# Layer 0's experts on gathered 256-row tiles between the scan tiles, and the end of layer 0 batch by batch

## The chip, the cores and the metric

The kernel runs on one core of a Trainium2 chip. A core has five engines that work side by side and meet through semaphores: TensorE (PE, matrix products), VectorE (DVE), ScalarE (ACT), GpSimd (POOL) and SyncE (SP), which here only issues transfers. Sixteen DMA engines carry the transfers of all of them. Each engine works off its own list of instructions in order. The metric is the device time of one execution in microseconds (us); the median of the runs is what counts, and lower is better.

## What is computed

Four layers, each of the form x + s(xn) * silu(g(xn)), where xn is the layer norm of x. Only layer 0 and the joint to layer 1 matter here. In layer 0, s is a selective scan (Mamba) and g a mixture of eight experts of which each row takes two:

```python
xz = x @ in_proj_w.T + in_proj_b              # x: 4 batches x 512 rows x 128
x_part, z = split(xz)                         # 256 channels each
x_conv = silu(causal_conv4(x_part))
dt = softplus(x_conv @ dt_w.T + dt_b);  Bm, Cm = x_conv @ B_w.T + B_b, x_conv @ C_w.T + C_b
h[t] = exp(dt[t] * A) * h[t-1] + dt[t] * Bm[t] * x_conv[t]     # 16 states per channel
y = (sum_s h[t] * Cm[t] + D * x_conv[t]) * silu(z);   s = y @ out_w.T + out_b

logits = xn @ gate_w + gate_b;  top 2 of 8, softmax over the two -> comb
h = gelu(xn @ w1[e] + b1[e])                  # 128 -> 512, exact GELU
g = sum_e comb[:, e] * (h @ w2[e] + b2[e])    # 512 -> 128
```

That is 2048 rows; each row needs two of the eight experts. Layer 1 is an attention of 16 heads beside four experts (again two per row).

## The kernel before

Everything is float32 in tiles of 128 partitions. The instructions of layer 0 are written in the order in which each engine is to take them (`manual_schedule`), so where a call stands in the loop decides what it waits behind.

**The scan loop.** The 4 batches x 256 channels x 16 states are cut into 128 tiles of 128 partitions (8 channels x 16 states) by 512 time steps, the tiles n = 0 to 127, 32 of them to a batch. A tile needs dt and dt*x of its 8 channels, each repeated 16 times over the partitions: two loads `rep` of 256 KB (`fetch`, L690, on SP) from the DRAM buffer `ddd`. ACT makes exp(A*dt) (`decay`, L696, tile `dA`), DVE multiplies B with the other load (`drive`, L703, `dBx`) and runs the recurrence (`scan`, L707, `hs`, two buffers), POOL multiplies by C (L709, `hc`). Every four steps `sum_states` (L718) has PE sum the states. `decay` runs LEAD + 1 = 6 steps ahead of the scan; the loads run AHEAD = 4 tiles ahead of their users, in 4 and 5 buffers. The next batch's projection, convolution and step sizes (`project_in`, `convolve`, `silus`, `in_stages`) and the last one's output (`gated`, `back`) are placed at set steps through `after(steps, fn, ...)`, a table of calls for later steps.

**The experts of layer 0.** `Experts` runs all eight experts on all rows: 32 steps of 512 rows (8 experts x 4 batches), two of them every eight scan steps. `hidden` (L562, L563) does four matmuls of 128 x 512 and four GELUs, `output` (L573) 16 matmuls of 128 columns, and `add_weighted` (L523) adds each of the four row blocks to `acc`, weighted with the gate. `weighted_bias` starts `acc` with the biases. ACT loads a table before the GELUs and another after them (`exp_ln`, L746).

**The end of layer 0.** `end_layer0` takes silu of all of `acc`, multiplies and adds into x; `begin_layer` norms all 16 row blocks and transposes them for layer 1.

**Layer 1.** Its four experts are already routed: class `Routed` computes each row's place (`route`), scatters the rows into the DRAM buffer `xs1` by 32 indirect transfers (L1257, on POOL), takes 19 tiles of 256 rows through their expert, whose weights come by an indirect load (L1270, on POOL), stores them to `ys` and gathers two rows per row again (`results`, L1346). Its stages run beside the attention through `Places`: `add` puts a chain of stages on a list, `work` and `place` run one stage each when its turn has come, `need` runs a chain to its end. The rows of `xs1` are filled with zeros by 19 stores at scan steps 40 to 58. At attention step PAUSE = 36 the attention stops for the experts.

Of the kernel before, what the change touches and what calls it, by code (L numbers as in the profile page):

```python
# [34 lines left out]
E0, FF0 = 8, 512  # L35
E1, FF1 = 4, 704
# [3 lines left out]
SLOT1 = 256  # L40
TILES1 = (2 * N - E1) // SLOT1 + E1
# [9 lines left out]
for _name, _n in (  # L51
    ("in_b", 4), ("conv_w", 2 * KCONV), ("conv_b", 2), ("dt_b", 2), ("A_log", 2 * STATE), ("D", 2),
    ("B_b", 1), ("C_b", 1), ("b1_0", E0 * 4), ("b1_2", E2 // 2), ("b1_3", E3 * 2), ("b2_3", E3), ("q_b", 1), ("k_b", 1),
):
    _COLS[_name] = (_at, _n)
    _at += _n
# [15 lines left out]
for _name, _n in (("before", P), ("ones", P), ("tile", TILES1), ("full", N // SLOT1), ("carry", E1 * NC), ("part", 1)):  # L72
    _RT[_name] = (_at, _n)
    _at += _n
# [3 lines left out]
def _constants():  # L78
# [24 lines left out]
    for name, v in (  # L103
        ("before", i[:, None] < i[None, :]), ("ones", 1.0), ("tile", np.arange(TILES1)),
        ("full", SLOT1 * np.arange(N // SLOT1)), ("carry", np.tile(np.arange(NC) > 0, E1)),
        ("part", i[:, None]),
    ):
        at, n = _RT[name]
        route[:, at : at + n] = v
# [40 lines left out]
def _layout(a):  # L150
# [26 lines left out]
    put("b1_0", chunked(a["L0_ffn_b1"].reshape(-1), E0 * 4))  # L177
# [38 lines left out]
    for i, w1, w2 in ((0, "w1", "w2"), (1, "w1", "w2"), (2, "w1", "w2"), (3, "W1", "W2")):  # L216
        out[f"f{i}_w1"], out[f"f{i}_w2"] = a[f"L{i}_ffn_{w1}"], a[f"L{i}_ffn_{w2}"]
# [11 lines left out]
def kernel(ctx: ExitStack, tc: tile.TileContext, ap: dict):  # L229
# [59 lines left out]
    xs1 = dram.tile([TILES1 * SLOT1, D], F32, name="xs1")  # L289
# [3 lines left out]
    nc.sync.dma_start(out=pick2, in_=ap["c_pick2"])  # L293

# [140 lines left out]
    def begin_layer(s):  # L435

        normalize(s, x)
        xnT = keep.tile([P, N], F32, name="xnT")
        transpose_chunks(xnT, s, NC)
        return xnT  # L440

    def end_layer0(s, y):

        act.activation(y, y, AF.Silu)
        half = NC // 2
        for h in range(2):
            cs = slice(h * half, (h + 1) * half)
            dve.tensor_tensor(s[:, cs, :], s[:, cs, :], y[:, cs, :], ALU.mult)
            dve.tensor_tensor(x[:, cs, :], x[:, cs, :], s[:, cs, :], ALU.add)

# [51 lines left out]
    def weighted_bias(acc, cw, b2, e, fp):  # L502

        for q in range(NC // 4):
# [3 lines left out]
            cwT = fp.tile([e, 512], F32, tag="cwT", name="cwT", bufs=1)  # L508
# [5 lines left out]

    def add_weighted(acc, py, cw, tb, e, first=False):

        for i in range(4):
            c = 4 * tb + i
            src = py[:, i * P : (i + 1) * P]
            if first:  # L520
                dve.tensor_scalar(acc[:, c, :], src, cw[:, c, e : e + 1], None, ALU.mult)
            else:
                dve.scalar_tensor_tensor(acc[:, c, :], src, cw[:, c, e : e + 1], acc[:, c, :], ALU.mult, ALU.add)  # L523


    def moe0_gate(xnT, scratch):
# [9 lines left out]
        yield cw  # L536

    class Experts:


        def __init__(self, fp, xnT, cw, acc):
            self.fp, self.xnT, self.cw, self.acc = fp, xnT, cw, acc
            self.steps = [(e, tb) for e in range(E0) for tb in range(4)]
            self.w, self.h = {}, {}

        def load(self, e):
            if e < E0 and e not in self.w:
                w1 = self.fp.tile([P, FF0], F32, tag="w1", name="w1")
                nc.sync.dma_start(out=w1, in_=ap["f0_w1"][e])
                w2 = self.fp.tile([P, 4, D], F32, tag="w2", name="w2")  # L550
                nc.sync.dma_start(out=w2, in_=ap["f0_w2"][e].rearrange("(f p) d -> p f d", p=P))
                self.w[e] = (w1, w2)

        def hidden(self, k):
            e, tb = self.steps[k]
            if tb == 2:
                self.load(e + 1)
            w1 = self.w[e][0]
            h = self.fp.tile([P, 4, 512], F32, tag="h", name="h", bufs=3)
            for f in range(4):  # L560
                ph = bank()
                pe.matmul(ph, w1[:, f * P : (f + 1) * P], self.xnT[:, tb * L : (tb + 1) * L], start=True, stop=True)  # L562
                act.activation(h[:, f, :], ph, AF.Gelu, bias=col("b1_0", e * 4 + f))  # L563
            self.h[k] = h

        def output(self, k):
            e, tb = self.steps[k]
            h, w2 = self.h.pop(k), self.w[e][1]
            py = bank("py")
            for i in range(4):  # L570
                cs = slice(i * P, (i + 1) * P)
                for f in range(4):
                    pe.matmul(py[:, cs], h[:, f, cs], w2[:, f, :], start=(f == 0), stop=(f == 3))  # L573
            return lambda: add_weighted(self.acc, py, self.cw, tb, e)


    def layer0(ctx0, mp, fp, s_out, acc):
# [23 lines left out]
        xnT = keep.tile([P, N], F32, name="xnT")  # L601
        at, n = _COLS["A_log"]
        A = mp.tile([P, n], F32, name="A")
        ln = tc.tile_pool(name="ln0", bufs=1)
        ln_pool = ln.__enter__()
        ln_close = lambda: ln.__exit__(None, None, None)
# [29 lines left out]
        def step_size(b, o):  # L636
# [6 lines left out]
            dd = mp.tile([P, 2, L], F32, tag="dd", name="dd", bufs=2)  # L643
# [498 lines left out]

# [646 lines left out]
```

## Time and profile before

| | us |
|---|---|
| runs, median of 3 (lowest to highest) | 1801.49 (1791.64 to 1809.43) |
| profiled execution, its own time | 1814.22 |
| its span, first to last instruction | 1812.5 |
| mean granted TensorE clock | 0.828 |
| busy PE, DVE, ACT, POOL over the span | 1373.3, 1143.7, 955.1, 536.2 |
| first scan instruction starts | 53.63 |
| last scan instruction ends | about 489 |
| first score row of layer 1 reduced on DVE | 531.91 |
| last scatter of layer 1's rows starts | 668.8 |
| layer 1's expert matmuls start | 691.9 |

How lines of the profile are read: a group names the line of the kernel, the engine, the operation, what is written and read and in what shapes, and how often; then the busy time in us and the mean of one in ns; then the idle time of the engine just before it, and who ended that. A wait reads: who waited, for whom, us in total, how often, the longest. A window row gives busy time and number of instructions for each engine. SPq is SP's DMA queue, PEld TensorE's weight loads.

### The profile page before, as it was taken

The page shows a single profiled execution, that of the slowest core. Times are in us where ns is not written, and L with a number is a line of the kernel's source. Part 1 is how long each engine was busy: PE and PEld are TensorE (multiplying, and loading weights), DVE is VectorE, ACT ScalarE, POOL GpSimd, SP SyncE. Part 2 cuts the span into 40 slices and gives each one's busy share as a digit, 9 for nine tenths or more (in the row PEclk, how much of TensorE's full clock was granted, in tenths as well). Part 3 has the DMA queues.
Part 4 walks back from the last instruction along what each step waited for, and adds up shares of the span by engine and source line. Part 5 has one row for each costly group of instructions (what it writes and reads, how often), then busy time and mean ns, then how long its engine had stood idle before and what let it go on. Part 6 is the DMA issues. An engine that isn't in the chain of part 4 may idle for free.

```text
span 1812.5 us, 22587 instructions
## 1 busy us (share of the span) xinstructions
PE 1373.3 (76%) x7845; PEld 699.2 (39%) x7845; DVE 1143.7 (63%) x1987; ACT 955.1 (53%) x1302; POOL 536.2 (30%) x513
## 2 busy tenths in 40 slices
PE   4678878788857888999586667776767877788771
PEld 2445445445532336888232222222312322233331
DVE  6467677677766664222466775657658799876422
ACT  3555655555524654223335777777885545354640
POOL 1245354444514652111534221214010101031223
PEclk8689889898857878999677877778868898598985
DMA  4557677576321231441302231220310211112112
GB/s 125 144 160 196 157 211 193 141 209 179 99 56 35 44 101 50 142 158 39 72 18 51 39 51 23 40 31 13 58 24 13 86 27 19 18 31 65 45 44 75
DMA packets 119122, 148.64 MB, mean 82 GB/s; under 512 B 15384, under 2 KB 79968, under 8 KB 117216
## 3 DMA queue, kind: packets, MB, share of 16 engines
q1 hardware_dynamic: 112048, 122.55, 28.7%
q0 software_dynamic: 6960, 24.65, 4.0%
q8 instruction: 62, 1.02, 0.2%
q14 instruction: 52, 0.43, 0.1%
HBM read 113.84 MB, written 16.01 MB: 72 GB/s over the span
## 4 chain that ended last, share of the span: by engine, by line
PE 43%; DVE 20%; ACT 15%; issue 10%; DMA 6%; POOL 3%; SPq 1%; POOLq 0%; DVEq 0%; ACTq 0%
PE wide L878 6%; PE py L1032 6%; PE wide L1313 5%; PE bank L562 5%; ACT at L1016 4%; PE py L573 4%; PE wide L885 3%; DMA rep<-ddd 3%; DVE nm L985 3%; PE py L1293 3%; ACT ep L980 3%; DVE den L981 2%; DVE hs L707 2%; PE wide L927 1%; ACT dA L696 1%
## 5 line engine op out<-in xcount | busy, mean ns | idle before, releaser
L1016 ACT ACTIVATE at<-wide 128x1024 f32<-128x1024 f32 (+3 forms) x384 | 352.5, 923 | 265.1 <-PE wide L885 175.6
L985 DVE TENSOR_REDUCE nm<-wide 128x2 f32<-128x1024 f32 (+3 forms) x256 | 256.8, 1019 | 105.1 <-PE wide L885 88.7
L1032 PE MATMUL py<-at,vaug 128*32 128x512 f32 (+3 forms) x1536 | 235.8, 671 | 11.7 <-POOL at L1020 8.5
L709 POOL TENSOR_TENSOR hc<-hs,C 128x512 f32<-128x512 f32 x128 | 163.2, 1279 | 250.3 <-DVE hs L707 145.1
L981 DVE TENSOR_REDUCE den<-ep 128x2 f32<-128x1024 f32 x128 | 155.5, 1217 | 115.0 <-ACT ep L980 114.3
L878 PE MATMUL wide<-k,q 48*128 48x512 bf16 (+4 forms) x768 | 167.9, 413 | 78.1 <-ACT at L1016 42.3
L562 PE MATMUL bank<-xnT,w 128*128 128x512 f32 x256 | 149.3, 738 | 75.7 <-ACT h L563 56.9
L980 ACT ACTIVATE ep<-wide 128x1024 f32<-128x1024 f32 x128 | 132.7, 1037 | 43.5 <-PE wide L878 33.9
L707 DVE TENSOR_TENSOR_SCAN hs<-dA,dBx 128x512 f32<-128x512 f32 x128 | 154.7, 1209 | 0.6 <-POOL hc L709 0.6
L573 PE MATMUL py<-w,h 128*128 128x128 f32 x1024 | 129.5, 288 | 19.6 <-DVE acc L523 19.6
L573 PEld LDWEIGHTS py<-w,h 128*128 128x128 f32 x1024 | 127.3, 204 | 38.6 <-DVE acc L523 27.9
L885 PE MATMUL wide<-own_bf 128*128 128x128 bf16 x880 | 138.8, 245 | 0.0
L696 ACT ACTIVATE dA<-rep,A 128x512 f32<-128x512 f32 x128 | 87.3, 715 | 97.6 <-DVE hs L707 69.4
L878 PE MATMUL wide<-q,k 63*128 63x512 bf16 (+3 forms) x512 | 101.9, 393 | 40.3 <-DVE nm L985 16.2
L703 DVE TENSOR_TENSOR dBx<-B,rep 128x512 f32<-128x512 f32 x128 | 89.0, 696 | 55.5 <-DMA rep<-ddd 35.8
L562 PEld LDWEIGHTS bank<-xnT,w 128*128 128x128 f32 x256 | 58.0, 237 | 166.6 <-ACT h L563 77.5
L878 PEld LDWEIGHTS <-q 48*128 48x128 bf16 (+1 forms) x768 | 49.8, 96 | 163.1 <-issue 145.3
L1313 PE MATMUL wide<-xT,w 128*128 128x256 f32 x456 | 108.5, 387 | 2.1 <-ACT h L1316 1.5
L1318 DVE TENSOR_TENSOR h<-h,wide 128x512 f32<-128x512 f32 x57 | 39.2, 688 | 110.5 <-ACT h L1316 110.5
L563 ACT ACTIVATE h<-bank,cols 128x512 f32<-128x512 f32 x128 | 84.7, 687 | 42.6 <-PE bank L562 42.2
L885 PEld LDWEIGHTS <-own_bf 128*128 128x128 bf16 x880 | 52.2, 101 | 113.8 <-issue 107.3
L878 PE MATMUL wide<-qr,kr 48*128 48x512 bf16 x256 | 61.3, 452 | 45.3 <-ACT ep L980 40.1
(324 smaller groups left out, 2086.7 us busy)
## 6 DMA issues: line engine op xcount, KB each, us to landing
rep<-ddd SPq DMA_DIRECT2D x256, 256.0 KB
q<-parts SPq DMA_DIRECT2D x192, 48.0 KB
k<-parts SPq DMA_DIRECT2D x192, 48.0 KB
w<-in_f_w_dram SPq DMA_DIRECT2D x18, 256.0 KB
ddd<-dd POOLq DMA_DIRECT2D x8, 512.0 KB
w<-in_f_w_dram SPq DMA_DIRECT2D x32, 128.0 KB
qr<-rparts SPq DMA_DIRECT2D x64, 48.0 KB
kr<-rparts SPq DMA_DIRECT2D x64, 48.0 KB
```

The source lines that it names most:

```text
L562: pe.matmul(ph, w1[:, f * P : (f + 1) * P], self.xnT[:, tb * L : (tb + 1) * L], start=True, stop=True)
L573: pe.matmul(py[:, cs], h[:, f, cs], w2[:, f, :], start=(f == 0), stop=(f == 3))
L707: dve.tensor_tensor_scan(h, st[n]["dA"], st[n]["dBx"], 0.0, ALU.mult, ALU.add)
L709: pool.tensor_tensor(hc, h, batch[tiles[n][0]]["C"], ALU.mult)
L878: pe.matmul(ps[:, j, lo:hi], lhs[m][r, cs], rhs[m][r, lo:hi], start=True, stop=not own)
L885: pe.matmul(ps[:, j, cs], lhs_own, rhs_own, start=False, stop=True)
L980: act.activation(e, ps, AF.Exp)
L981: dve.tensor_reduce(s["den"][:, qc, 2 * m : 2 * m + 2], e, AX.X, ALU.add)
L985: dve.tensor_reduce(s["nm"][:, qc, 2 * m : 2 * m + 2], ps[:, :, :hi], AX.X, ALU.max, negate=True)
L1016: act.activation(a[:, :, lo:], ps[:, :, lo:], AF.Exp)
L1032: pe.matmul(s["po"][32 * j : 32 * j + 32, lo:], vaug[b % 2][:, kc, 4 * g + j, :], a[:, j, lo:], start=kc == 0, stop=kc == 3,)
L1313: pe.matmul(ph[:, g, m * SLOT1 : (m + 1) * SLOT1], wk[:, f + g, m, :], self.x[k], start=True, stop=True)
```

## The change

Layer 0's experts are routed as layer 1's are. `Routed` becomes a common class, with `Routed0` and `Routed1` for what differs; its own table of constants is loaded at the start. Layer 0 has 23 tiles of 256 rows (the most that 4096 choices over eight experts can need). The scratch `xs` is shared by both layers and filled with zeros once, by one transfer at the start, issued by POOL. In the scan loop:

- the route stages run one per step from step 0, then the 32 scatters, one per step (`places.work()` is called twice per step); `places.need("rows")` at step 43 makes sure of them, and the first two tiles are loaded there;
- from step FIRST = 46, two tiles every five steps: rows transposed by PE and copied by ACT, then both first layers, then the second layers in the two steps after, each with a copy on ACT and a store on SP. Loads of the next tiles (weights by POOL, rows by SP) stand one and three steps after the pair begins;
- from step DONE = 108 the results of the batches one after the other, a stage per step: two stages of four gathers, then the weighted sum on DVE onto the biases in `acc`, and silu in three stages; after each, `turn` multiplies, adds into x, norms and transposes that batch. Batch 3's results come after the loop, and the turns of batches 2 and 3 in layer 1's first attention steps.

Layer 1's routing waits until all four turns are over. `end_layer0`, `begin_layer`, `Experts` and `add_weighted` go. `hc` has 6 buffers instead of 8 and `dd` one instead of two; `sum_states` runs at n % 4 == 1 instead of 3.

```diff
+    xs = dram.tile([TILES0 * SLOT, D], F32, name="xs")
+    pool.dma_start(
+        out=xs.rearrange("(p k) d -> p k d", p=P), in_=zero[:, None, :].to_broadcast([P, TILES0 * SLOT // P, D])
+    )
...
+        def load(self, k):
+            if k < self.tiles:
+                pool.indirect_dma_start(
+                    out=self.w[k % len(self.w)], out_offset=None, in_=self.weights,
+                    in_offset=bass.IndirectOffsetOnAxis(ap=self.expert[:, k : k + 1], axis=0),
+                    bounds_check=self.e * P - 1, oob_is_err=False,
+                )
+                self.x[k] = self.wp.tile([P, 2, D], F32, tag="xr", name="xr", bufs=3)
+                nc.sync.dma_start(
+                    out=self.x[k], in_=xs[k * SLOT : (k + 1) * SLOT, :].rearrange("(h p) d -> p h d", p=P)
+                )
...
+        def results(self, b, y, room, biased=False):
+            ya = room()
+            yb = room() if biased else None
+            own = lambda c: yb[:, c, :] if biased else y[:, 4 * b + c, :]
+            for c in range(4):
+                self.gather(own(c), 0, 4 * b + c)
+                self.gather(ya[:, c, :], 1, 4 * b + c)
+                if c % 2:
+                    yield 0
+            yield 0
+            for c in range(4):
...
+                if biased:
+                    dve.scalar_tensor_tensor(yc, own(c), w[0], yc, ALU.mult, ALU.add)
...
+                dve.scalar_tensor_tensor(yc, ya[:, c, :], w[1], yc, ALU.mult, ALU.add)
+            yield 0
+            yield from silu(b, y, ya)
...
+    class Routed0(Routed):
...
         def hidden(self, k):
...
+            w = self.w[k % len(self.w)]
+            h = self.h[k] = self.fp.tile([P, NF0, SLOT], F32, tag="h", name="h", bufs=2)
+            for f in range(0, NF0, 2):
                 ph = bank()
+                for g in (f, f + 1):
+                    pe.matmul(ph[:, (g - f) * SLOT : (g - f + 1) * SLOT], w[:, g * P : (g + 1) * P], self.x[k], start=True, stop=True)
+                for g in (f, f + 1):
+                    b1 = w[:, FF0 + NF0 * D + g : FF0 + NF0 * D + g + 1]
+                    act.activation(h[:, g, :], ph[:, (g - f) * SLOT : (g - f + 1) * SLOT], AF.Gelu, bias=b1)
...
-            hc = st[n]["hc"] = sp.tile([P, L], F32, tag="hc", name="hc", bufs=8)
+            hc = st[n]["hc"] = sp.tile([P, L], F32, tag="hc", name="hc", bufs=6)
...
+        FIRST = 46
+        DONE = FIRST + (TILES0 + 1) // 2 * 5 + 2
...
         def experts(k):
-            after(0, ex.hidden, k)
-            after(0, ex.hidden, k + 1)
-            for i in range(2):
-                after(1 + 4 * i, lambda k: after(3, ex.output(k)), k + i)
+            pair = [n for n in (k, k + 1) if n < TILES0]
+            for n in pair:
+                after(0, ex.turned, n, act.copy)
+                after(1, ex.hidden, n)
+                after(2 + n - k, ex.output, n, FF0, NF0)
+                after(1 + 2 * (n - k), ex.load, n + 2)
+            after(1, exp_ln)
...
+            places.add("route", (1 for _ in ex.route(sel, cw)))
+            places.add("rows", ex.scatter(s_out), after="route")
...
+                places.now += 1
+                if n == FIRST - 3:
+                    places.need("rows")
+                    for k in range(2):
+                        ex.load(k)
+                if n >= FIRST and (n - FIRST) % 5 == 0 and (n - FIRST) // 5 * 2 < TILES0:
+                    experts((n - FIRST) // 5 * 2)
...
+                if n == DONE:
+                    for k in range(B):
+                        places.add(("y0", k), ex.results(k, acc, room, True), after=("y0", k - 1))
+                    turns(0, 1)
...
-                if 0 <= n - 40 < TILES1:
-                    nc.sync.dma_start(
-                        out=xs1[(n - 40) * SLOT1 : (n - 39) * SLOT1, :].rearrange("(h p) d -> p h d", p=P),
-                        in_=zero[:, None, :].to_broadcast([P, 2, D]),
-                    )
...
-                if n % 4 == 3 and n > 3:
+                if n % 4 == 1 and n > 3:
                     sum_states(n // 4 - 1)
...
+                for _ in range(2):
+                    places.work()
...
             back(B - 1)()
+            for k in range(B):
+                places.need(("y0", k))
+            turns(3)
...
+            while not places.over.issuperset((0, b) for b in range(B)):
+                yield "free"
...
-    end_layer0(s, acc)
...
-        xnT = begin_layer(s)
```

## The prediction

> **What bounds the kernel now.** I read the windows by stretch first, since the change touches only layer 0 (the first 530 us of 1812.5), then the waits inside the scan loop, then the groups, for durations. The stretches are cut at starts of the scan instruction (L707), one per step n = 0 to 127; the columns are the stretch, its length, busy us of PE, PEld, DVE, ACT and POOL, the granted TensorE clock, the DMA share and GB/s.
>
> ```profile
> 53.63:66.79 13.16, 9.47 (x20) 4.10 (x20) 10.95 (x13) 11.15 (x15) 8.18 (x7) 0.79 0.58 152
> 66.79:187.72 120.93, 97.83 (x444) 60.67 (x445) 77.72 (x110) 66.04 (x95) 51.98 (x43) 0.84 0.60 161
> 187.72:230.84 43.12, 32.23 (x170) 20.27 (x169) 27.97 (x43) 26.01 (x37) 14.90 (x12) 0.91 0.61 160
> 230.84:432.75 201.91, 163.06 (x772) 97.46 (x772) 147.40 (x205) 114.11 (x158) 99.40 (x82) 0.89 0.68 188
> 432.75:487.69 54.94, 48.47 (x276) 31.46 (x275) 40.70 (x61) 31.45 (x42) 24.77 (x20) 0.92 0.58 145
> 487.69:531.91 44.22, 21.93 (x108) 15.20 (x108) 22.54 (x70) 12.55 (x16) 14.95 (x19) 0.63 0.17 43
> ```
>
> These are n = 0-4, 5-36, 37-45, 46-107, 108-127 and the way to layer 1's first score row. A step takes 3.4 us on average, but DVE is busy only 70% of that. The reader should see that no engine is full: the loop stalls. The waits in the loop say on what:
>
> ```profile
> POOL hc L709 <- PE y L718: 77.0, 16, 8.9
> ACT dA L696 <- DVE hs L707: 69.4, 40, 4.8
> ...
> DVE acc L523 <- PE py L573: 35.9, 13, 17.0
> DVE dBx L703 <- DMA rep<-ddd: 35.8, 31, 2.8
> ```
>
> The DMA queue's own list of waits begins with
>
> ```profile
> SPq L690 <- ACT dA L696: 229.9, 62, 13.7
> ```
>
> PE runs the experts in program order ahead of the state sums, so POOL waits for a buffer; ACT spends about 10 us on eight GELUs paced by PE, the decays behind them are late, and SP cannot issue the next rep loads until a decay frees a buffer (229.9 us). The expert blocks stall the scan. Undisturbed steps follow each other at 1.85 us, which is one scan and one drive back to back:
>
> ```profile
> L562 PE MATMUL bank<-xnT,w 128*128 128x512 f32 x256 | 149.3, 738 | 75.7 <-ACT h L563 56.9
> ...
> L707 DVE TENSOR_TENSOR_SCAN hs<-dA,dBx 128x512 f32<-128x512 f32 x128 | 154.7, 1209 | 0.6 <-POOL hc L709 0.6
> L573 PE MATMUL py<-w,h 128*128 128x128 f32 x1024 | 129.5, 288 | 19.6 <-DVE acc L523 19.6
> ...
> L703 DVE TENSOR_TENSOR dBx<-B,rep 128x512 f32<-128x512 f32 x128 | 89.0, 696 | 55.5 <-DMA rep<-ddd 35.8
> ```
>
> **What the change removes.** 32 tiles of 512 rows become 23 of 256: 36% of the expert columns. PE's 279 us (149.3 + 129.5) fall to about 100; ACT's GELUs from 84.7 us to 92 x 0.47 = 43 (0.47 interpolated between 393 ns for 160 columns, L1595, and 687 for 512, L563); the 128 weighted adds on DVE (35.5 us) go. After that DVE needs 1.85 us a step plus, per batch of 32 steps, convolution 7, step sizes 4.5, gating 1.5: about 2.3 us a step.
>
> **What it adds, by stretch.** The three resources that can take PE's place are POOL, the DMA engines and DVE.
>
> *Before the loop:* POOL zero-fills 3 MB of xs at once, beside the first input loads. At 276 GB/s (the 188 GB/s of the long stretch over its share 0.68) that is 11 us of DMA, in a start where the share is 0.50 over 53 us. Nothing in the trace shows a 5888-row fill by POOL. Ends: 0 (hidden) and +12 (all of it ahead of the loads). I take +4.
>
> *n = 0-4:* routing moves here: some 30 small DVE operations of 0.2-0.3 us (layer 1's own route, L1187-L1253), 7 us, and one matmul round trip that DVE waits for, 2 us. 13 becomes 22: **+9**. The bias matmuls stay; their 13 us on ACT are covered by the five steps that the decays lead.
>
> *n = 5-36:* one scatter a step on POOL, 32 in all. A scatter waits for the one before to land, because both write xs, and it stands in POOL's queue ahead of the next hc; hs has two buffers, so two steps later the scan waits for POOL. Layer 1's scatters show the price:
>
> ```profile
> 602.31 0.99 POOL L1257 DMA_INDIRECT xs<-acc,pos  x1 [1.73 <-DMA xs<-acc,pos]
> ...
> 605.28 0.99 POOL L1257 DMA_INDIRECT xs<-acc,pos  x1 [1.19 <-DMA xs<-acc,pos]
> ...
> 607.83 0.99 POOL L1257 DMA_INDIRECT xs<-acc,pos  x1 [0.77 <-DMA xs<-acc,pos]
> ...
> 610.37 0.99 POOL L1257 DMA_INDIRECT xs<-acc,pos  x1 [0.75 <-DMA xs<-acc,pos]
> ```
>
> They start 2.5 to 3.0 us apart, up to 3.5 elsewhere, with the DMA engines nearly idle. The Trainium skill's "DMA: Bandwidth & Descriptors" (Anatomy of one DMA, SWDGE path) gives about 2.0 us fixed plus bytes over 436 GB/s: 2.15 us for these 64 KB, so POOL itself would be the pace, (1.27 + 1.3) x 32 + 12 for step sizes and gating = 94 us. By the rows, with some delay for rep traffic, 3.2 us a step: 32 x 3.2 + 5 for POOL's heavy steps = 107. I take the rows: 120.9 to 107, **-14**. Ends 94 and 145 (4.4 us a step): no row has a scatter under a half-full DMA load.
>
> *n = 37-45:* no experts at all. Nine steps at 1.85, one batch's convolution 7.4 and the odd step-size operation: 26 for 43.1, **-17**. The stall by the experts goes, DVE is late next; rep loads need about 2.0 us a step, just under it.
>
> *n = 46-107:* two tiles every five steps. DVE would want 62 x 2.3 = 143 us. ACT per five steps: 5 decays 3.6, 8 GELUs 3.8, four copies of 256 columns 1.5 (0.373 each, L1295), two table loads 2.6, batch work 1.9: 13.4, or 2.7 a step, 166 us. DMA: 124 rep loads of 256 KB 32.5 MB; weights of 526 KB each for the tiles loaded here, 18 that move (counts of the seed-0 inputs give 20 real tiles, and three of 23 loads find their expert already there) 9.5 MB; xr and ys 5.8 MB; ddd 2 MB: 49.8 MB. At 276 GB/s this is 180 us. The skill's same page (Specifications) puts the HBM limit per core near 358 GB/s, which would be 139 us and leave ACT as the bound; it also warns that transfers issued from POOL and SP share the same 16 engines. The row decides on the rate, since these are the very 2 KB rows that dominate. So the DMA engines become the bound here: 182 for 201.9, **-20**. Ends 155 and 205. SP's ys store waits for ACT's copy with rep issues behind it, but those wait for decays behind the same copy. POOL's load of tile k+3 waits for PE's output k, finished about a step earlier. Two cuts I cost at nothing: hc has 6 buffers for 8, so each third or fourth step waits for state sums queued one step before (their cover; if PE is late with a pair's first layer, some 2 us a pair, 24 in all, inside the ends); dd has one for two, with four steps between its uses.
>
> *n = 108-127:* results of batches 0 to 2: 24 gathers at 1.3 us start to start (L1346, 858.67 to 859.98) 31 us, 20 hc 25, clip and multiply 8, turns and gating 6: POOL 70, DVE 58. With a little waiting 72 for 54.9, **+17**. Four gathers at a time hold hc back for 5.2 us, and there the scan waits.
>
> *To layer 1's first score:* whole-array SiLU, layer norm and transposes (490 to 513 us) go. In their place POOL does one batch's eight gathers, clip and multiply (16 us), and only then the 7.4 us of memsets for vaug and q (L1661), which the value copy and the q rows need. 44.2 becomes 42: **-2**. The first projection is early, the memsets are late next.
>
> *Layer 1:* its routing now waits for turns of batches 2 and 3, four or five attention steps later. Its last scatter was at 668.8 and the expert matmuls began at 691.9, so 15 us of delay nearly fit: **+3**, ends 0 and +12.
>
> **Sum:** 4 + 9 - 14 - 17 - 20 + 17 - 2 + 3 = -20 us. The profiled execution took 1814.2 (span 1812.5), 13 over the median; as a difference it goes onto the median: 1801.5 - 20 = **1781 us**. A measurement of this kernel can tell about 1%, 18 us, from no change.
>
> **Rivals.**
>
> *The scatter chain (slower, 0.35).* With rep loads in the same DMA engines a scatter lands later, and every step of n = 5-36 waits. For: the same-buffer wait is real in layer 1 and the scan hangs on hc. Against: the scatters pace the scan, which itself thins the rep traffic to 60%. At 4.6 us a step the stretch is 152 instead of 107: 1781 + 45 = 1826. It loses the whole gain from 3.8 us a step, and 1% of the kernel from 4.4.
>
> *DMA stays loose (faster by much, 0.15).* If the rates of the best slices hold, n = 46-107 runs at ACT's and DVE's pace, 155, and the scatters at POOL's, 94: 1781 - 27 - 13 = 1741. For: slices of the loop reach 300 GB/s. Against: at the loop's start, with nothing but rep loads, a pair took 2.12 us, 247 GB/s.
>
> *DMA is tighter (no change, 0.2).* At 250 GB/s the long stretch takes 200, its old length: 1799. The MoE's freed PE time is then hidden behind transfers.
>
> *The forecast (faster, 0.3).* A change that doesn't route would show 32 expert tiles; the diff leaves 23 fixed, so I give that nothing.
>
> **How the numbers follow.** Faster by over 1%: 0.3 + 0.15 = 0.45; within 1%: 0.2; slower by over 1%: 0.35. The range reaches from below the loose case to above the scatter case: 1735 to 1835. Its lower part also holds a better start and tail, its upper part the fill's +12 and layer 1's +12 with a milder scatter.
>
> **What would show it.** PE busy in the loop (351 us) falls under 200, acc adds vanish. Scatter starts in n = 5-36 lie 3.0 to 3.5 us apart and the waits list "POOL xs <- DMA xs"; at 4.4 the first rival is right, at 2.9 the second. In n = 46-107 the DMA share is 0.9 or more at about 2.9 us a step; a share under 0.8 at that pace means another cause. n = 108-127 shows four gathers and a scan gap of 5 us. If layer 1's expert matmuls start later after the first score than the old 160 us by over 12, my layer 1 term is wrong. The sum fails if PE or ACT waits still fill the loop.

## The result, and the profile after

The change makes the kernel slower: 1869.3 us median of four runs (1863.4 to 1872.0) against 1799.9 of the kernel before beside it, a ratio of 1.038 (95% interval 1.032 to 1.044). The forecast was 1781. The profiled execution took 1872.0 us, with a span of 1870.0.

The same stretches as before, by windows (stretch, length, busy us of PE, PEld, DVE, ACT, POOL, granted clock, DMA share, GB/s): the start, n = 0-4, 5-36, 37-45, 46-107, 108-127, and the way to the first score.

```profile
0.00:60.65 60.65, 23.21 (x72) 12.90 (x72) 29.42 (x84) 20.07 (x29) 7.21 (x12) 0.83 0.57 178
60.65:82.53 21.88, 16.19 (x57) 11.04 (x58) 21.19 (x42) 9.36 (x16) 11.12 (x9) 0.50 0.38 111
82.53:196.68 114.15, 61.40 (x96) 10.98 (x94) 72.00 (x80) 36.67 (x53) 80.90 (x71) 0.66 0.62 184
196.68:228.12 31.44, 19.32 (x47) 5.61 (x47) 29.02 (x29) 13.96 (x21) 17.73 (x15) 0.72 0.60 168
228.12:445.74 217.62, 155.26 (x788) 107.86 (x788) 129.47 (x145) 138.40 (x247) 123.31 (x104) 0.86 0.88 229
445.74:526.40 80.66, 25.37 (x46) 3.97 (x46) 58.31 (x100) 14.61 (x25) 57.18 (x50) 0.57 0.46 115
526.40:577.55 51.15, 14.06 (x38) 6.74 (x37) 8.71 (x15) 10.26 (x15) 28.32 (x31) 0.57 0.17 44
```

| stretch | before | after | difference | predicted |
|---|---|---|---|---|
| to the first scan | 53.6 | 60.7 | +7.0 | +4 |
| n = 0-4 | 13.2 | 21.9 | +8.7 | +9 |
| n = 5-36 | 120.9 | 114.2 | -6.8 | -14 |
| n = 37-45 | 43.1 | 31.4 | -11.7 | -17 |
| n = 46-107 | 201.9 | 217.6 | **+15.7** | -20 |
| n = 108-127 | 54.9 | 80.7 | **+25.7** | +17 |
| to the first score | 44.2 | 51.2 | +6.9 | -2 |
| the rest (span less first score) | 1280.6 | 1292.5 | +11.9 | +3 |
| sum | | | +57.4 | -20 |

PE is far from busy in n = 5-36 and 108-127, as intended, and the loop has not become faster for it. In n = 46-107, with 36% of the old expert columns, the stretch is longer than with all of them. Its longest waits but for those on the scan itself (who waits for what: us in total, times, longest):

```profile
PE bank L644 <- DMA xr<-xs: 42.6, 10, 8.8
DVE dBx L895 <- DMA rep<-ddd: 42.0, 22, 5.6
...
ACT xT L646 <- PE bank L644: 31.6, 9, 7.9
```

and SP's own list, where before the whole wait stood on the rep issue:

```profile
SPq L658 <- ACT yt L657: 92.2, 22, 11.0
SPq L882 <- ACT dA L888: 13.4, 12, 2.4
```

PE waits for an expert tile's rows, ACT's xT copy waits for PE, and the decays stand behind that copy in ACT's order. SP spends 92 us waiting with a tile's store (ys, L658) at the head of its queue.

Stretches of untouched code differ a little between runs: n = 46-107 took 211 to 218 us in nine profiles with the same instructions there, mean 214.4; n = 5-36 took 112 to 123. An edit's gain is read against these, or against a run on the same chip.

### The profile page after: what moved, and what is told of

The parts are those of the page before. It is cut to its first block, busy times and chain, and to the rows that moved or that the text cites. A ratio compares the mean times of both kernels' runs of the same rounds, so it can differ in the third digit from the quotient of the medians.

```text
span 1870.0 us, 21518 instructions
## 1 busy us (share of the span) xinstructions
PE 1299.7 (70%) x7169; PEld 623.2 (33%) x7169; DVE 1143.7 (61%) x1931; ACT 916.7 (49%) x1322; POOL 644.9 (34%) x613
## 4 chain that ended last, share of the span: by engine, by line
PE 31%; DVE 15%; issue 11%; ACT 10%; POOL 5%; DMA 4%; SPq 1%; POOLq 0%; DVEq 0%; ACTq 0%
PE py L1248 7%; PE wide L1094 6%; PE wide L757 5%; ACT at L1232 4%; PE wide L1101 3%; DVE nm L1201 3%; DVE den L1197 2%; PE py L655 2%; ACT ep L1196 2%; PE wide L1143 1%; PE bank L1621 1%; PE bank L456 1%; DMA room<-ys,pos 1%; DMA rep<-ddd 1%; PE bank L1265 1%
## 5 line engine op out<-in xcount | busy, mean ns | idle before, releaser
L910 PE MATMUL y<-hc,cst 128*32 128x512 f32 x256 | 106.8, 807 | 93.1 <-POOL hc L901 70.9
L655 PE MATMUL py<-w,h 128*128 128x128 f32 x824 | 101.2, 278 | 9.7 <-ACT yt L657 8.2
L655 PEld LDWEIGHTS py<-w,h 128*128 128x128 f32 x824 | 98.3, 192 | 20.2 <-ACT yt L657 11.7
L1094 PE MATMUL wide<-qr,kr 48*128 48x512 bf16 x256 | 62.0, 459 | 45.3 <-ACT ep L1196 40.1
L757 PEld LDWEIGHTS wide<-xT,w 128*128 128x128 f32 x456 | 83.3, 193 | 15.6 <-issue 3.4
L631 POOL DMA_INDIRECT w<-in_f_w_dram,expert x42 | 43.8, 1042 | 123.4 <-PE py L655 116.7
```

Source lines behind the costliest of these rows:

```text
L655: pe.matmul(py[:, cs], h[:, f, cs], w[:, at + f * P : at + (f + 1) * P], start=(f == 0), stop=(f == nf - 1))
L757: pe.matmul(ph[:, g, m * SLOT : (m + 1) * SLOT], wk[:, f + g, m, :], self.x[k], start=True, stop=True)
L910: pe.matmul(t["y"][32 * q : 32 * q + 32, :], ysel[:, m, :], st[4 * k + q]["hc"], start=m == 0, stop=m == 3)
L1094: pe.matmul(ps[:, j, lo:hi], lhs[m][r, cs], rhs[m][r, lo:hi], start=True, stop=not own)
```

## Experiments: the expert steps, n = 46-107

My first theory was that SP's queue is blocked: the store waits for ACT, and rep and xr loads stand behind it. The rivals were the DMA rate, and ACT's order. Three single edits, and after them their combinations, tell these apart.

**The store moved to ScalarE's queue** (edit in short form).

```diff
-            nc.sync.dma_start(out=self.ys[...], in_=yt...)
+            nc.scalar.dma_start(out=self.ys[...], in_=yt...)    # layer 0 only
```

> The store of each layer-0 expert tile's output (ys) is issued from ScalarE's queue, right behind the copy that it waits for, and no longer from SP's. Theory A (SP's queue is blocked: stores that wait for ACT's copy, 92 us in 22 waits, hold back the rep and xr loads queued behind them): the 92 us vanish, the waits of PE on xr (42.6 us) fall under 15 and those of DVE on rep (42.0 us) under 25; steps 46 to 107 fall from 217.6 us to about 185 (the 50 MB at 270 GB/s), the kernel from 1869 to about 1838. Rival B (the DMA engines' rate is the bound): the same bytes in the same time, 213 to 220 us, the kernel within 6 us of 1869. Rival C (ACT's own order is the bound: table loads, GELUs and decays in a queue): no change or a little slower, since ACT gets 23 more instructions to issue.

Measured: ratio 1.034 (1.028 to 1.041); the stretch 208.4 us at 239 GB/s, by its window:

```profile
226.76:435.19 208.43, 151.06 (x788) 105.38 (x788) 129.53 (x146) 140.40 (x247) 123.30 (x104) 0.89 0.88 239
```

SP's list of waits in this stretch now begins

```profile
SPq L882 <- ACT yt L657: 70.7, 12, 10.9
SPq L882 <- ACT dA L888: 26.1, 23, 5.2
```

The wait for the yt copy is still there, now on the rep issue itself (L882): the rep load needs a buffer that a decay frees, and the decay stands behind that copy on ACT. The theory asked for 185 us, and for waits of PE on xr under 15 us; they are still 27.4. It falls as stated, though the stretch is 6 us under the mean of the unchanged profiles and below all nine of them: while the rows come late, the store's place may matter a little.

**Fewer weights.** The weight load of a layer-0 tile is issued only for k < 3.

> Only the first three layer-0 weight loads are made; tiles 3 to 22 compute with the weights already there, so their results are those of other experts. About 9 MB of 50 MB in steps 46 to 107 are not moved and POOL issues 20 DMAs (22 us) fewer. Theory A (SP's queue): the stores still block SP, steps 46 to 107 stay over 205 us (217.6 before), the kernel over 1855. Rival B (DMA rate): 41 MB at 229 to 255 GB/s, 160 to 180 us, the kernel near 1825. Rival C (ACT's order): 212 to 218 us.

Measured: ratio 1.025 (1.019 to 1.031); the stretch 199.2 us, DMA share 0.77, 206 GB/s. 9 MB less win 15 us of 214.4, where a pure DMA bound at 250 GB/s would give 36. None of the three theories alone explains that.

**The rows earlier** (edit in short form).

```diff
-                self.x[k] = self.wp.tile([P, 2, D], F32, tag="xr", name="xr", bufs=3)
-                nc.sync.dma_start(out=self.x[k], in_=xs[k * SLOT : ...])
+            self.rows_in(k + 2)        # five buffers; the first two tiles' rows with the first loads
```

> The rows xr of each layer-0 tile are loaded two tiles further ahead (five buffers for three), with the stores still on SP's queue. Theory A: PE's waits on xr (42.6 us) go under 10, but SP stays blocked by the stores and the rep loads stay late; steps 46 to 107 fall by 10 to 25 us, the kernel to 1845 to 1860. Rival B (DMA rate): the same bytes, 213 to 220 us; the waits move from xr to rep. Rival C: within 5 us of 217.6.

Measured: ratio 1.028 (1.022 to 1.034); the stretch 200.0 us, with the store still on SP's queue:

```profile
226.53:426.52 199.99, 150.65 (x788) 102.51 (x788) 129.51 (x145) 138.63 (x247) 123.26 (x104) 0.91 0.91 250
```

The waits on xr are gone from the list, and this stays the costliest wait of DVE and PE on a load:

```profile
DVE dBx L903 <- DMA rep<-ddd: 34.0, 19, 5.2
...
PE bank L713 <- DMA w<-in_f_w_dram,expert: 20.1, 7, 7.2
```

while SP's own list still begins with the store:

```profile
SPq L666 <- ACT yt L665: 83.1, 23, 10.3
```

So 83 us of a waiting queue cost next to nothing, and the lateness of one kind of load that stands in it cost 15 us (214.4 less 199.5, the mean of this run and two below with the same edit).

**Both.**

> Both at once: the layer-0 stores of ys issued from ScalarE's queue and the rows xr loaded two tiles further ahead. Steps 46 to 107 took 217.6 us in the changed kernel, 208.4 with the stores moved alone, 200.0 with the rows early alone, where the DMA share was 0.91 at 250 GB/s. If blocked and late transfers on SP's queue are all that is wrong, the two gains add: about 188 us, 265 GB/s, kernel near 1845. If the DMA engines' rate is the bound once the rows come early: 196 to 201 us at a share of 0.91 to 0.95, kernel 1850 to 1857.

Measured: ratio 1.027 (1.021 to 1.033); the stretch 199.5 us, share 0.91, 249 GB/s. The gains do not add. Once the rows are early, it does not matter whose queue the store stands in; what is left looks like the DMA rate.

**Both, and fewer weights.**

> As the run with stores on ScalarE's queue and rows early, and only the first three layer-0 weight loads are made, so tiles 3 to 22 compute with other experts' weights: 9 MB of 50 MB less in steps 46 to 107. If the DMA rate is then the bound, the stretch goes to 41 MB over 250 GB/s, about 165 us, at a share still near 0.9. If ScalarE's order or the lockstep of ScalarE, VectorE and PE is the bound (ScalarE is busy 138 us and VectorE 130 us of the stretch, with table loads and waits for each other), it stays over 183 us and the DMA share falls under 0.8.

Measured: ratio 1.016 (1.010 to 1.022); the stretch 180.6 us, share 0.85, 226 GB/s. Its window:

```profile
223.84:404.43 180.59, 144.47 (x788) 101.09 (x788) 130.49 (x146) 138.88 (x247) 101.51 (x84) 0.94 0.85 226
```

In between: without 9 MB another limit is met 15 us ahead of the DMA rate's 165.

**No table loads.** With the rows early, GELU replaced by Exp and `after(1, exp_ln)` taken out.

> Layer 0's rows xr are loaded two tiles further ahead, as in the run that took 200.0 us for steps 46 to 107 at 250 GB/s, and the experts' GELU is replaced by Exp, so that ScalarE makes no table loads for them (about 24 of 1.28 us, 31 us, fall away in the stretch); the results are those of another function. If the DMA rate is what is left as the bound: 195 to 200 us. If ScalarE's order is: 170 to 182 us at more than 270 GB/s. Taking 9 MB of weights away gave 180.6 us with both; a fall here to about 188 would say that both hold by turns.

Measured: ratio 1.022 (1.020 to 1.025). The window of the stretch:

```profile
232.85:425.05 192.20, 149.43 (x788) 102.60 (x788) 130.26 (x145) 108.72 (x223) 123.67 (x104) 0.91 0.96 258
```

ACT does 30 us less and the stretch shrinks by 7, up to a DMA share of 0.96 at 258 GB/s. That is close to a pure DMA bound: 192 us for these bytes. The 7 us between 199.5 and 192.2 are then what ACT's table loads cost: with them the same bytes come at a share of 0.91. This rests on one profile, against three with the rows early that lie between 199.1 and 200.0.

## Experiments: the steps before and the end

**Half the scatters.** `for a in range(1)` for 2 in layer 0's scatter.

> In layer 0 only each token's row for its first expert is scattered (16 scatters for 32), so the other rows of the tiles stay zero and their results are wrong; layer 1 is as before. Steps 5 to 36 took 114.2 us with 32 scatters about 3.6 us apart. If the chain of scatters is the pace there: 16 steps at 3.6 and 16 at what VectorE needs, 2.3 to 2.6, about 97 us, and the kernel about 17 us less than 1869. If VectorE's own work (72 us busy) and the late step sizes set the pace, no less than 108 us.

Measured: ratio 1.025 (1.019 to 1.031); n = 5-36 took 100.6 us, where three kernels with all scatters took 112.1 to 116.7 on the same chip: 14 us for 16 scatters. POOL's list of waits in this stretch of the changed kernel says why a scatter costs that:

```profile
POOL xs L623 <- DMA xs<-s,pos: 17.4, 18, 2.5
```

and DVE's list for the same stretch:

```profile
DVE hs L899 <- POOL hc L901: 28.3, 21, 3.9
```

The scatter waits for the one before it, and the scan waits for the hc behind the scatter.

**Two tensors.** The second choices' rows go to a tensor that nobody reads, so that neighbouring scatters do not wait for each other (edit in short form).

```diff
-                        out=xs[:, :], out_offset=self.at(a, c), ...
+                        out=(xs_b if a else xs)[:, :], out_offset=self.at(a, c), ...   # layer 0 only
```

> Layer 0's scatters of the second choices go to a tensor of their own that nobody reads (those rows stay zero in the tiles, their results are wrong); scatters then alternate between two tensors, 32 as before. If a scatter's wait for the landing of the one before is the pace of steps 5 to 36 (114 us in the changed kernel, 118 to 123 on the chip of the last runs): it falls to 98 to 104, as with half the scatters (100.6). If POOL's issue of the scatters or the DMA traffic itself is: no more than 5 us.

Measured: ratio 1.026 (1.022 to 1.031). The window of n = 5-36, and the wait of the scan that is left (from 81 to 190 us):

```profile
81.27:175.78 94.51, 55.37 (x96) 9.98 (x94) 73.47 (x80) 36.33 (x53) 81.18 (x71) 0.75 0.74 219
```

```profile
DVE hs L900 <- POOL hc L902: 12.7, 15, 3.9
```

94.5 us for 120.3 of the changed code on the same chip (in the run with the end made at once), with the same 32 scatters and the same POOL busy time (81 us). The wait for the scatter before to land is the pace, and costs some 20 to 26 us of this stretch. No version that routes rightly without that wait was tried.

**The fill just ahead of the loop, and in it.** The zero fill of xs moved from the kernel's start to just ahead of `places.add("route", ...)`, and in another kernel to the end of step 1 (`after(0, ...)` at n == 1, with the rows early as well).

> The zero fill of xs (3 MB) is issued just ahead of the scan loop and not at the kernel's start. Before the change the first scan started at 53.6 us, with it at 59.2 to 60.7. If the fill's traffic beside the first input loads costs that: 53.5 to 56 us to the first scan, with at most 3 us given back in steps 0 to 4 (21.9 us), where POOL's issue of 2.3 us now lies. If the gate's work moved ahead of the loop costs it: 59 to 60.7 stays.

Measured: ratio 1.041 (1.038 to 1.044), no gain: the first scan at 60.6 us. The timeline of ACT shows both halves of it. The first input copy (xpad) of the changed kernel, and of this one:

```profile
23.84 0.69 ACT L809 ACTIVATE xpad<-bank,cols 128x512 f32<-128x512 f32 x1 [10.75 <-PE bank L808]
```

```profile
16.32 0.69 ACT L806 ACTIVATE xpad<-bank,cols 128x512 f32<-128x512 f32 x1 [5.70 <-PE bank L805]
...
46.05 0.72 ACT L885 ACTIVATE dA<-rep,A 128x512 f32<-128x512 f32 x1 [16.21 <-DMA rep<-ddd]
```

Away from the start the fill frees the input loads (7.5 us earlier), and then the first decay waits 16.2 us for its rep load, 10.8 in the changed kernel: the fill has moved beside the next transfers that somebody waits for.

> Rows xr two tiles further ahead, and the zero fill of xs issued at the end of step 1 of the loop, where the DMA share was 0.38. If the fill costs only where the DMA engines are wanted: the first scan starts at 53.5 to 55 us for 59 to 61, steps 0 to 4 stay near 22 to 24, and the ratio to the kernel before is about 1.023 (1.0278 with the rows early alone). If the fill's time comes back in steps 0 to 10 (POOL's issue, later rep loads, first scatter waiting for it): 1.027 again.

Measured: ratio 1.027 (1.024 to 1.030); first scan at 53.4 us, n = 0-4 23.2. The start's 7 us are won, but n = 5-36 took 125.8, so nothing was seen in the total. Whether the 7 us came back there, or the chip was slow in that stretch, was open; the pair of kernels at the end bears on it.

**The gathers apart.** A `yield 0` after each gather.

> In layer 0 each gather of a batch's results is one place's work of its own, not four in a row: two a step on POOL, with the next state product hc between them. If the gaps of 9 to 12 us in the scan of steps 108 to 127 come from four gathers in a row ahead of hc: the stretch falls from 80.7 to about 68, at the price of fewer batches done before the loop ends (more left for the tail: its 51 us grow by up to 16), the kernel 1855 to 1872. If POOL's total work sets the stretch, no change in the sum of both stretches (131.8 us).

Measured: ratio 1.034 (1.027 to 1.040). n = 108-127 fell from 80.7 to 53.2 and the way to the first score grew from 51.2 to 80.6: the sum is 133.8 for 131.8. No gain; what is not done in the loop is done after it.

**The memsets on VectorE.** `dve.memset` for `pool.memset` of vaug and q.

> The memsets of vaug and q ahead of layer 1 (7.6 us on POOL, at 553 us, behind batch 3's gathers, clip and multiply) are made on VectorE. If they are what layer 1's projection waits for: PE's wait on them (21 us) is gone or short, the way from the last scan to the first score falls from 51.1 us to about 42. If something beside them (batch 3's back projection, turn or the first weights) is as late: it stays over 48.

Measured: ratio 1.039 (1.036 to 1.041); the way 52.0 us. From its waits:

```profile
PE wide L1143 <- DVE vaug L1673: 21.9, 1, 21.9
...
DVE vaug L1667 <- POOL acc L1368: 5.5, 1, 5.5
```

PE waits as long as before, for the other engine's memset, which itself cannot begin before batch 3's last multiply (L1368). What is late is batch 3's chain of gathers, SiLU and multiply; the memset's engine is not the matter. The run with four repairs below, which has these memsets too, agrees: there this multiply starts 14.1 us after the start of the last scan instead of 25.5, and the way is 11 us shorter than in the changed kernel.

**The turns at once.** After `turns(3)`, `places.need((0, k))` for all four batches.

> At the end of layer 0 the turns (residual, norm, transpose) of batches 2 and 3 are made at once, ahead of layer 1, instead of one stage per attention step. Layer 1's first scatter came 18 us after its first score before the change and 55 us after it with it. If the late turns are the cause of layer 1's 11.9 us: the rest after the first score falls from 1292.5 to about 1281, the first expert matmul from 180 us after the first score to 160, and the way to the first score grows by 5 to 10 us. If something else in layer 1 is the cause, the rest stays over 1288 and the kernel gets slower by the added way.

Measured: ratio 1.034 (1.028 to 1.040). The way grew to 64.1 us (+13); the first expert matmul came 160.5 us after the first score, as before the change (160), for 180 in the changed kernel. The matmuls of layer 1's experts (shortest, median and longest in ns, then first and last start in us), in the changed kernel and in this one, whose first scores are at 577.6 and 588.3 us:

```profile
L757 PE MATMUL wide<-xT,w x456: 378/379/793, 757.6 to 916.3; 128*128 128x256 f32 x152
```

```profile
L757 PE MATMUL wide<-xT,w x456: 379/379/795, 748.8 to 908.7; 128*128 128x256 f32 x152
```

The rest took 1285.6 us, where three kernels with late turns took 1307.6 to 1313.3 on the same chip. The late turns are the cause of layer 1's loss. Making them at once costs 12 to 13 us on the way and wins 22 to 28 behind it by these profiles, 7 by the changed kernel's own; in the ratios (1.034 for 1.038) the gain is within the intervals.

**The end made at once.** No `results` and `turns` in the loop; after it 32 gathers, the weighted sums, one SiLU, residual, norm and transposes.

> The routed experts as in the changed kernel, but nothing of the end in the loop: all 32 gathers, the weighted sums, one SiLU, residual, norm and transposes after it, as the kernel before made its end. Steps 108 to 127 then hold POOL's hc alone: 80.7 to about 52. The way to the first score: 32 gathers at 1.3 us (42 us), the memsets 7.6, and 40 us of SiLU, norm, transposes and first projections: 51 to about 90. Layer 1: experts 160 us after the first score for 180, 7 to 12 us less. If staging the end hid most of its work: the sum is 10 us or more slower than the changed kernel. If it hid nothing in the end: within 5 us of it or faster.

Measured: ratio 1.028 (1.026 to 1.031). Windows of n = 108-127 and of the way to the first score:

```profile
445.76:484.48 38.72, 22.95 (x37) 2.75 (x38) 34.96 (x41) 10.67 (x14) 24.49 (x20) 0.74 0.86 199
484.48:578.20 93.72, 21.09 (x86) 13.39 (x85) 34.42 (x100) 12.64 (x16) 45.77 (x51) 0.58 0.16 41
```

132.4 us in all, for 131.8 with the staged end. Staging hid nothing. The 19 steps of the stretch take 2.04 us each with DVE busy 35.0 of 38.7, so there was no room on DVE; put into them, the work of three batches lengthened them by 42 us, and the way after them shrank by the same.

**Four repairs together.**

> The changed kernel with four things mended together: rows xr two tiles further ahead (-17 us), the zero fill just ahead of the loop (-5), the memsets for layer 1 on VectorE (-8), and the expert tiles started at step 41 for 46, so that five more steps of the loop are there for the gathers (-5). If the four add: 35 us less than the changed kernel's 1869, ratio to the kernel before 1.015 to 1.02, still slower. If what is won is given back in another stretch: ratio over 1.025.

Measured: ratio 1.028 (1.024 to 1.032), 18 and 22 us better than the two kernels on the same chip with the memsets or the fill moved alone (1876 and 1880), hardly more than the rows alone bring. The way fell to 40.1 us, but n = 37-107 took 252.6, where it was 230.5 with the rows early alone: the five steps that now held gathers (n = 103-107) took 20.5 us for 9.8, and the 62 expert steps, started earlier, 214 for 200. Won there, given back here.

**The bytes spread.** Rows early, the end at once, FIRST = 41, and pairs of tiles every seven steps.

> Rows two tiles further ahead, the end made at once after the loop, and the pairs of expert tiles every seven steps from step 41 for every five from step 46, so that the same bytes go through the DMA engines over steps 41 to 121. Steps 37 to 127 took 329.7 us in the changed kernel and 283.3 with the end at once. They need 63 MB: at 258 GB/s, the rate of the fullest stretch seen, 244 us; VectorE needs about 215. If the DMA rate is what bounds the expert steps: 245 to 260 us, and the ratio to the kernel before 1.005 to 1.015. If the tiles stall the scan by waits of their own, wherever they lie (23 tiles by some 4 us): 275 us or more, and over 1.02.

> The same with the zero fill of xs issued at the end of step 1. It saved 6 us ahead of the first scan before, and steps 0 to 36 took 149.0 us for 142.2 in another kernel on the same chip. If the fill's DMA time comes back there: within 3 us of the kernel with the fill at the start. If that was the chip: 5 to 7 us less.

> The changed kernel itself, as the measure for the two others on the same chip: ratio 1.032 to 1.044 as before; steps 5 to 36 between 114 and 123 us, and steps 46 to 107 between 208 and 218.

| kernel | median us | ratio (95%) | first scan | n = 5-36 | n = 37-127 | way to score |
|---|---|---|---|---|---|---|
| spread | 1846.5 | 1.023 (1.020 to 1.026) | 60.1 | 119.3 | 270.2 | 93.2 |
| spread, fill in the loop | 1843.7 | 1.021 (1.018 to 1.024) | 52.5 | 118.1 | 272.1 | 94.3 |
| the changed kernel again | 1876.3 | 1.039 (1.036 to 1.043) | 59.4 | 118.2 | 323.8 | 53.1 |

Spreading took n = 37-127 to 270.2 us from 283.3 with the end at once, between the two expectations: the DMA rate's 245 to 260 was not reached, and the ratio, 1.023, is the second's. None of these 13 us can be put down to spreading: the rows early are worth as much alone (309 to 311 us for these steps in three profiles, for 324 and 330 in the changed kernel's two). The window of n = 46-107 in the first of them, where the DMA engines are still nearly full:

```profile
240.66:426.17 185.51, 130.37 (x624) 82.89 (x625) 131.59 (x145) 117.59 (x208) 119.33 (x100) 0.86 0.93 250
```

The fill at step 1 starts the scan 7.6 us earlier and costs 1.3 us in n = 0-4 and nothing seen in n = 5-36 (118.1 for 119.3), so up to there it does not come back. The two profiled executions still took the same time (spans of 1842.5 and 1842.2): the 7.5 us are gone again in small pieces of the same code later on. In the medians the gain is 2.8 us, with overlapping intervals, which is the expectation's first branch. That the fill is cheaper there is shown up to step 36, not for the kernel.

The best version is 1.7% faster than the changed kernel and still 2.1% slower than the kernel before. Against the profile before (span 1812.5, 13 us over its median), it has -1.2 to the first scan, +10.1 in n = 0-4, -2.8 in n = 5-36, -27.7 in n = 37-127, +50.1 on the way to the first score, +1.4 behind it. That is the balance of the change once its waits are mended: the routed experts save about 30 us in steps 5 to 127, routing costs 10 ahead of them, and to fetch and finish their results costs 50 behind them. No run beat the kernel before.

## Why the prediction was wrong

**n = 46-107 (36 us off, the largest error).** The sentence that failed is "So the DMA engines become the bound here: 182 for 201.9, -20". My own ends for it, 155 and 205, do not hold the 217.6 either. Three terms were off. The first is a wait that was not in the sum. I argued that SP's waiting store costs nothing, "those wait for decays behind the same copy", and for the rep loads the runs agree: with the rows early the stretch takes 200.0 us with the store on SP's queue and 199.5 without. But I counted only the rep loads behind that store. The rows xr of the coming tiles stand in the same queue, with three buffers and two to four steps of lead. They came up to 9 us late: 15 us.

The second is the rate: I took 276 GB/s, the long stretch's 188 over its share. The fullest stretch seen moved 258 at a share of 0.96: 192 us, so 10 more. More of that is the share than the rate: 258 over 0.96 is 269, but no stretch here filled the engines to 1. The bytes were right (49.8 MB estimated, 229 GB/s for 217.6 us are 49.8), and they are 12 MB more than the kernel before moved there (188 GB/s for 201.9 us: 38.0).

The third is that the bound was taken as if it were always fed; ACT's table loads break it: 7. From 182 this leads to 214, the mean of the unchanged profiles. With the rows early the stretch is what my third rival said, 200 us at 250 GB/s. Of the cuts that I had costed at nothing, hc's six buffers held: POOL's hc waited 4.7 us for PE in this stretch, where it waited 33.5 before.

The Trainium skill ("DMA: Bandwidth & Descriptors", Issuing engines are not separate DMA queues) says that issuing from several engines saves only the issue time; the run with both edits agrees, 199.5 us for 200.0. It does not speak of what a waiting transfer holds up behind it in its engine's queue, which here was the rows.

**n = 5-36 (-7 for -14).** The mechanism was as written: scatters pace the scan through hc, each waiting for the one before. The size was off: on average they start 3.75 us apart (85.3 to 201.5 us, 31 intervals), where I took 3.2. Three of them in POOL's timeline (start, length, instruction, idle time before it, what ended that):

```profile
89.70 1.04 POOL L623 DMA_INDIRECT xs<-s,pos  x1 [2.05 <-DMA xs<-s,pos]
...
94.83 1.43 POOL L623 DMA_INDIRECT xs<-s,pos  x1 [1.90 <-DVE xc L815]
...
99.15 1.00 POOL L623 DMA_INDIRECT xs<-s,pos  x1 [1.58 <-DMA xs<-s,pos]
```

A convolution on DVE (xc) holds a scan, and with it POOL, between two scatters; these delays add to the landing waits and do not hide in them. By what ended the wait, 20 of the 31 intervals were set by a landing; they are 2.5 to 4.8 us long, median 3.1, close to the 3.2 that I took. The other 11, ended by DVE, by ACT or by POOL's own step-size work, average 4.5. The first rival asked for scatters that land later beside rep loads: layer 1's landings in the kernel before set intervals of 2.5 to 3.6 us, and only six of the 20 are longer. So its mechanism had a small part. The term that I sized wrong is the 5 us for heavy steps: these 11 intervals exceed 3.2 us by 1.3 each, 14 in all.

**n = 37-45.** Predicted 26, measured 31.4: DVE is busy 29.0 of it, 3 us more than I counted for the batch's work. The last scatters still fall in here; with half of them the nine steps took 27.2.

**n = 108-127 (+26 for +17).** I added POOL's work up to 70 us and took 72. POOL was busy only 57, of 80.7. I saw that the scan waits behind the gathers, and did not cost that DVE has no time to catch up: its queue holds the next drive and scan behind the turn's operations, which wait for POOL. POOL's timeline of the changed kernel, behind a block of four gathers that began at 505.3 us:

```profile
510.31 1.27 POOL L901 TENSOR_TENSOR hc<-hs,C 128x512 f32<-128x512 f32 x1
511.53 1.27 POOL L1376 TENSOR_TENSOR s<-s,acc 128x512 f32<-128x512 f32 x1
```

and DVE's at the same time:

```profile
512.83 0.69 DVE L1378 TENSOR_TENSOR x<-x,s 128x512 f32<-128x512 f32 x1 [6.22 <-POOL s L1376]
...
516.22 1.20 DVE L899 TENSOR_TENSOR_SCAN hs<-dA,dBx 128x512 f32<-128x512 f32 x1
```

Four gathers on POOL, then hc and the turn's multiply, and only then DVE's residual add, its norm statistics and the next drive: between the scan at 505.4 and the next at 516.2 lie 10.8 us, where I had 5.2.

**To the first score (+7 for -2).** I saw the memsets as late next. Put on another engine, they were as late: the chain of batch 3 before them is the step I had left without a price. **Layer 1 (+12 for +3)** is the end of my own range: the first scatter came 55 us after the first score for 18 before, and the expert matmuls 180 after it for 160, beyond the 12 that I had named as the sign of a wrong term.

**The start (+7 for +4)** was inside my ends and **n = 0-4 (+8.7 for +9)** was right, for the reason given: DVE is busy 21.2 of 21.9 us there, 10 more than before.

Of the signs, the scatters' distance pointed to the first rival's side, and a DMA share of 0.88 at 3.5 us a step (217.6 over 62) fitted neither branch: I had foreseen 0.9 or more at 2.9 us. PE's busy time in the loop, 277.6 us (16.2 + 61.4 + 19.3 + 155.3 + 25.4), did not fall under 200: the expert lines are busy 120 of it for the 100 that I took, and the state sums (L910) 103, where they showed 32 before.

## What to carry to other kernels

When a wait at the head of a queue is called free, go through everything behind it: here the loads that shared its cause lost nothing, and one other load behind it, with few buffers, stalled PE, ACT and with them the scan. Work put into a loop is hidden only if every engine it uses has time there, DVE's order included; compare the loop without it (2.04 us a step, DVE busy 90%) before counting on it. And a transfer that "runs beside" others costs its full time wherever somebody waits for the DMA engines next: the same 3 MB fill cost 7 us at the start, as much just ahead of the loop, and 1.3 us in steps 0 to 4, where the share was 0.38; that the whole kernel gains by this was not seen.

## What the runs showed of the hardware

Where PE had less to do, its granted clock fell: in n = 5-36 PE went from 81% busy to 54% and the clock from 0.84 to 0.66, in n = 108-127 from 88% to 31% and from 0.92 to 0.57. A state-sum matmul (L718, now L910) took 807 ns on average for 605 by the profile. PE's busy share is not the whole of it: in n = 0-4 it was 72% before and 74% after, and the clock 0.79 and 0.50. The Trainium skill ("TensorE: Matmul & The Clock Gate", The HAM clock gate) says that the clock follows PE's recent activity; less PE work is then not all gain. What the lower clock cost the path, no run here measures.
